# A twelve-block network on one core: layernorms by the statistics instruction, a rearranged delta rule, and narrow attention on single PSUM banks

## The chip, the core and the metric

The kernel runs on one core of a Trainium2 chip, in one launch. The metric is device time in microseconds for one execution, from inputs in HBM to the output in HBM. All arithmetic of interest here is float32.

## What is computed

A batch of 4 sequences of 128 tokens with 128 channels, `x`, goes through twelve blocks; each takes the layernorm of `x` and adds its result to `x`. A context of 4 x 2048 positions with 96 channels feeds three cross attentions. In order:

1. an attention and feed-forward with ternary weights and rounded inputs (`bit_attention`),
2. a selective state space block (`mamba`),
3. a grouped feed-forward,
4. a cross attention with 12 heads (`ctx_attention`),
5. the delta rule block (`rwkv`),
6. a mixture of 8 experts (`moe`),
7. a cross attention with 8 heads,
8. a causal attention with position biases (`alibi_attention`),
9. a ternary feed-forward (`bit_ffn`),
10. a cross attention with 8 heads of 16 channels (`narrow_attention`),
11. a causal attention with one head,
12. a routed feed-forward with gates.

The delta rule is the block with most of the change. Cut to what matters:

```python
x = _ln(x, ln_pre_w, ln_pre_b); xn = _ln(x, ln_attn_w, ln_attn_b)
dx = _shift(xn) - xn                       # xr, xw, xk, xv, xa, xg = xn + dx * x_r, ...
r, k, v = xr @ W_r, xk @ W_k, xv @ W_v
w_log = -softplus(-(w0 + tanh(xw @ w1) @ w2)) - 0.5
a = sigmoid(a0 + xa @ a1 @ a2);  g = sigmoid(xg @ g1) @ g2
kk = (k * k_k).reshape(.., 16, 8);  kk = kk / max(norm(kk), 1e-12)     # per head
k = k * (1.0 + (a - 1.0) * k_a)
def step(state, inp):                      # one token; state is 8 x 8 per head
    sa = einsum('bhij,bhj->bhi', state, a_t)          # a_t = -kk
    state = state * d_t + sa * b_t + v_t * k_t        # d = exp(-exp(w_log)), b = kk * a
    return state, einsum('bhij,bhj->bhi', state, r_t)
o = group_norm_of_heads(o) * gn_w + gn_b
o = o + (r * k * r_k).sum(head) * v
x = x + (o * g) @ W_o
xf = _ln(x, ln_ffn_w, ln_ffn_b); kf = xf + (_shift(xf) - xf) * ffn_x_k
x = x + square(relu(kf @ W_ffn1)) @ W_ffn2
```

A layernorm takes (x - mean) / sqrt(var + eps) over the last axis, times a weight and plus a bias where there are any. In `moe`, `bit_ffn` and `rwkv` a layernorm without weights is followed directly by one with weights.

## The kernel before

Tokens lie on the 128 partitions and (batch, channel) along the free axis, so `x` is a tile of 128 x 512; `transposed` turns it by four TensorE transposes into one PSUM bank and copies it out, with channels on the partitions. `copy` alternates between ScalarE and VectorE.

The program is written with pools of tiles. A pool has a number of buffers for each tag, and the tiles of one tag go round in them. Pools that are closed give their memory to the pools opened after them, in SBUF and in PSUM (8 banks of 512 float32 per partition). Every wait between engines comes from tiles that are written, read or given up. The order on each engine is set by a list scheduler: it follows the order of the program, but lets a later instruction go ahead where an earlier one isn't ready by its own estimate. Weights are loaded by SP through a pool of two buffers, a block ahead (`nxt()`).

**Layernorm** (`layernorm`, L330 to L351): sum (DVE, L335), mean (L337), centred copy (L339), square (POOL, L341), sum (L343), root (ACT, L345), reciprocal (L347), product (L348), and with weights two more passes (L350, L351).

**Delta rule** (`rwkv`): 784 to 973.6 us of the profile. Three layernorms; `transposed`; `shifted` copies the transpose into a padded tile and subtracts; six mixtures (`mixed`) each feed a matrix product (`mm`, tag "mm", four banks). The keys' head lengths go through a sum over heads and a reciprocal of all 512 columns (L1412). The sequence is cut in 32 blocks of 4 tokens (`NB`, `Q`). `products` (L1464) multiplies two operands, on DVE or POOL, in tag "pr" (two buffers) and sums over heads on PE. `spread` copies one of the 8 state columns to all channels of its head by a product with a constant. Tiles `br`, `ae` and `pt` hold what the 32 steps need; each step is four small DVE operations (L1545 to L1550) that depend on one another. Then the output: products of r with kh and v (L1554, `oa`), of r with be and `sa` (L1564), and for each of 8 columns `spread(rh, j)` times the state at the block's start (`oz`, also in tag "pr"), summed in `o_ps` by four products with the identity (L1584). After that come the group norm (a call of `layernorm`), its weights, the bonus term (`bo_ps`, `bs`, `vtok`), the gate `g`, W_o, and the feed-forward.

**Narrow attention**: keys kT and values v of one batch are projected from the transposed context (`project`, 8 key products of 512 columns, 16 value products of 136). For each batch b and each half of the heads s (four heads, one per group of 32 partitions), `maxima` computes all scores, four heads x 512 columns at a time, and reduces them on DVE (L709, L714); the row maxima are transposed (`m_tr`, L720) and added to the queries. `weighted` then computes transposed scores (L733, `t_ps`), takes the exponential on ACT (L739) and sums values on PE (L746, `av`), in four steps of four chunks. The loop runs `weighted` of (b, s) beside `maxima` of the next half and `project` of the next batch, one step of each in turn; `finish` normalises and multiplies by W_o. All score and projection tiles share tag "sc": three double banks. Small transposes have a bank of their own ("mi").

Of the kernel before, what the change touches and what calls it, by code (L numbers as in the profile page):

```python
# [18 lines left out]
P = 128  # L19
# [36 lines left out]
for _n, _w in [  # L56
    ("b_d2v", 1), ("b_img", 1), ("b_txt", 1), ("b_att0", 1), ("b_att1", 1), ("b_f1", 4),
    ("conv_w", 16), ("conv_b", 4), ("dtp_b", 4), ("D", 4), ("A_log", 64),
    ("x_r", 1), ("x_w", 1), ("x_k", 1), ("x_v", 1), ("x_a", 1), ("x_g", 1),
    ("w0", 1), ("a0", 1), ("k_k", 1), ("k_a", 1), ("r_k", 1), ("ffn_x_k", 1),  # L60
    ("moe_b1", 32), ("moe_gate", 8), ("b_q", 1), ("b_k", 1), ("b3_q", 1), ("b3_k", 1), ("router", 8), ("bq3", 2), ("inv_n", 7),
]:
    COLS.add(_n, _w)
# [3 lines left out]
for _n, _w in [  # L67
    ("b_f2", C), ("ln_pre_w", C), ("ln_pre_b", C), ("ln_attn_w", C), ("ln_attn_b", C),
    ("ln_ffn_w", C), ("ln_ffn_b", C), ("gn_w", C), ("gn_b", C), ("gamma", C), ("beta", C),
    ("b_v", C), ("b_out", C), ("ln1_g", C), ("ln1_b", C), ("ln2_g", 512), ("ln2_b", 512),  # L70
    ("b1", 512), ("b2", C), ("b3_v", C), ("bo1", C), ("bo2", C), ("bo3", C),
]:
    ROWS.add(_n, _w)
# [73 lines left out]
def _layout(i):  # L147
# [23 lines left out]
    for n in ("x_r", "x_w", "x_k", "x_v", "x_a", "x_g", "w0", "a0", "k_k", "k_a", "ffn_x_k"):  # L171
        col[n] = chunks(i["L1_attn_" + n])
    col["r_k"] = chunks(i["L1_attn_r_k"].reshape(-1))
# [12 lines left out]
    for n in ("ln_pre_w", "ln_pre_b", "ln_attn_w", "ln_attn_b", "ln_ffn_w", "ln_ffn_b", "gn_w", "gn_b"):  # L186
        row[n] = i["L1_attn_" + n]
    for n in ("gamma", "beta"):
        row[n] = i["L1_ffn_" + n]
# [81 lines left out]
class Net:  # L271
# [58 lines left out]
    def layernorm(self, pool, x, out, eps=0, w=None, b=None, tag="ln"):  # L330
# [3 lines left out]
        s = self.small(n, tag + "_s")  # L334
        nc.vector.reduce_sum(s, x, axis=AX)  # L335
        m = self.small(n, tag + "_m")
        nc.vector.tensor_scalar_mul(m, s, 1.0 / d)  # L337
        xc = pool.tile([P, n, d], F32, tag=tag + "_xc", name=tag + "_xc")
        nc.vector.tensor_sub(xc, x, bc_in(m, d))  # L339
        sq = pool.tile([P, n, d], F32, tag=tag + "_sq", name=tag + "_sq")  # L340
        nc.gpsimd.tensor_mul(sq, xc, xc)  # L341
        v = self.small(n, tag + "_v")
        nc.vector.reduce_sum(v, sq, axis=AX)  # L343
        sd = self.small(n, tag + "_sd")
        nc.scalar.activation(sd, v, AF.Sqrt, bias=self.eps[:, eps : eps + 1], scale=1.0 / d)  # L345
        r = self.small(n, tag + "_r")
        nc.vector.reciprocal(r, sd)  # L347
        nc.vector.tensor_mul(out, xc, bc_in(r, d))  # L348
        if w is not None:
            nc.vector.tensor_mul(out, out, bc_mid(w, n))  # L350
            nc.vector.tensor_add(out, out, bc_mid(b, n))  # L351

    def transposed(self, psum, pool, x, tag, dtype=F32):

        nc = self.nc
        ps = psum.tile([P, B, P], F32, tag="mm", name="tr_" + tag)
        for b in range(B):
            nc.tensor.transpose(ps[:, b], x[:, b], self.ident)  # L358
        out = pool.tile([P, B, P], F32, tag=tag, name=tag)
        self.copy(out, ps)  # L360
        return out

    def normed(self, psum, pool, tag="xn"):

        xn = pool.tile([P, B, C], F32, tag=tag, name=tag)
        self.layernorm(pool, self.x, xn)
# [90 lines left out]
    def ctx_attention(self, n, heads, mask, bo, nxt):  # L457
# [4 lines left out]
        with ExitStack() as es:  # L462
# [10 lines left out]
            self.layernorm(wk, self.x, xn)  # L473
# [154 lines left out]

    def narrow_attention(self, nxt):
# [7 lines left out]
        wqo, wkv = self.load("qo3"), self.load("kv3")  # L637
        scale = 1.0 / math.sqrt(ND)
        with ExitStack() as es:
# [7 lines left out]
            self.layernorm(one, self.x, xn)  # L647
            nc.vector.tensor_add(self.x, self.x, bc_mid(self.row("bo3"), B))
            tr = mi.tile([P, B, P], F32, tag="mi", name="tr_x")
# [24 lines left out]
            def project(b):  # L674

                kT = wk.tile([P, 2, S], F32, tag="kT", name="kT")
                v = wk.tile([P, NCH, NH * VW], F32, tag="v", name="v")
                for at in range(0, S, 512):
                    mm = ps.tile([P, 2, 512], F32, tag="sc", name="k_ps")
                    for s in range(2):  # L680
                        nc.tensor.matmul(  # L681
                            mm[:, s], wkv[:, s * P : s * P + P],
                            self.ctxT[: DC + 1, b * S + at : b * S + at + 512], start=True, stop=True)
                    self.copy(kT[:, :, at : at + 512], mm)
                    yield kT, v
                for c in range(0, NCH, 6):
                    mm = ps.tile([P, 2, 512], F32, tag="sc", name="v_ps")
                    n = min(6, NCH - c)
                    for j in range(n):
                        at = b * S + (c + j) * P  # L690
                        w = NH * VW
                        nc.tensor.matmul(
                            mm[:, j // 3, j % 3 * w : j % 3 * w + w], self.ctxT[: DC + 1, at : at + P],
                            wkv[:, 2 * P : 2 * P + w], start=True, stop=True)
                    for j in range(0, n, 3):
                        k = min(3, n - j)
                        self.copy(
                            v[:, c + j : c + j + k].rearrange("p c w -> p (c w)"), mm[:, j // 3, : k * w])
                    yield kT, v

            def maxima(b, s, kT):
# [3 lines left out]
                for j in range(4):  # L705
                    ts = [ps.tile([P, 2, 512], F32, tag="sc", name="s_ps") for _ in range(2)]
                    for g in (0, 2, 1, 3):
                        lo = g * 32
                        nc.tensor.matmul(  # L709
                            ts[g // 2][:, g % 2], qs[lo : lo + 32], kT[lo : lo + 32, s, j * 512 : j * 512 + 512],  # L710
                            start=True, stop=True)
                    for i, t in enumerate(ts):
                        at = j * 4 + i * 2
                        nc.vector.tensor_reduce(part[:, at : at + 2], t, axis=AX, op=ALU.max, negate=True)  # L714
                    yield
# [3 lines left out]
                tr = mi.tile([P, B, P], F32, tag="mi", name="m_tr")  # L719
# [5 lines left out]
            def weighted(b, s, kT, v, av):  # L725

                qs = q[:, s, b * T : b * T + T]
                for c0 in range(0, NCH, 4):
# [20 lines left out]

                    while late:  # L750
# [4 lines left out]
            def finish(b, av):  # L755
# [3 lines left out]
                tr = mi.tile([P, B, P], F32, tag="mi", name="o_tr")  # L759
# [7 lines left out]
                tr = mi.tile([P, B, P], F32, tag="mi", name="on_tr")  # L767
# [3 lines left out]
                y = mi.tile([P, B, P], F32, tag="mi", name="y")  # L771
# [9 lines left out]
            for kv in project(0):  # L781
                pass
            run(maxima(0, 0, kv[0]))
            done = None
            for b in range(B):
                av = avp.tile([P, 2, P], F32, tag="av", name="av")
                more = iter(project(b + 1)) if b + 1 < B else iter(())
                ahead = []
                for s in range(2):
# [4 lines left out]
                    for i, _ in enumerate(weighted(b, s, *kv, av)):  # L794
# [1223 lines left out]
```

## Time and profile before

| | |
|---|---|
| median of 3 runs | 1609.14 us (1604.18 to 1609.59) |
| profiled execution | 1603.5 us, span 1601.5 us, granted TensorE clock 0.842 |
| PE busy | 1180.8 us (74%) |
| DVE busy | 996.6 us (62%) |
| ACT busy | 625.3 us (39%) |
| POOL busy | 178.0 us (11%) |
| chain that ended last | PE 54%, DVE 15%, ACT 3% of the span |

A row of a group reads: line, engine, operation, output<-inputs, output form<-input form, count, then busy us and mean ns of one, then the engine's idle time just before it and what ended most of it. A row of the timeline reads: start in us, us, engine, line, operation, and in brackets the idle time before. A row of a window reads: its ends, its length, busy us (and number of instructions) of PE, PEld (weight loads), DVE, ACT and POOL, the granted clock, the DMA share and GB/s. Each float32 matmul appears as two records.

### The profile page before, as it was taken

What the parts mean: (1) busy time and instruction counts of PE and PEld (TensorE: products, weight loads), DVE (VectorE), ACT (ScalarE), POOL (GpSimd) and SP (SyncE); (2) the same over time, 40 slices, a digit from 0 to 9 for tenths busy, and PEclk for the clock granted to TensorE, in tenths of its full rate; (3) what the DMA queues carried; (4) which work ended last, traced back from release to release, by engine and by line L of the source; (5) the groups of instructions that cost most, each with busy time, mean ns of one, the idle gap of its engine ahead of it and who ended that gap; (6) DMA issues with size and microseconds to landing.
All of it is one profiled execution on the core that took longest, in us unless ns stands there. A gap on an engine that the chain in (4) does not pass through costs nothing.

```text
span 1601.5 us, 15594 instructions
## 1 busy us (share of the span) xinstructions
PE 1180.8 (74%) x6178; PEld 630.4 (39%) x6178; DVE 996.6 (62%) x1535; ACT 625.3 (39%) x786; POOL 178.0 (11%) x154
## 2 busy tenths in 40 slices
PE   2577356676999999999457055989775069989858
PEld 0266122224544444444223033754344035555534
DVE  8987478993376676676567954126676754344335
ACT  4722255551466565565333001436422113333242
POOL 0047023561000000000002000000030000000000
PEclk9988558798899999999759576989986578889778
DMA  5000000007000000000010005000000000000010
GB/s 163 1 2 2 0 1 26 1 0 192 1 0 1 0 1 0 0 0 1 0 53 0 0 1 155 1 20 0 2 1 9 0 1 2 1 1 2 6 50 7
DMA packets 9371, 28.19 MB, mean 18 GB/s; under 512 B 1175, under 2 KB 7104, under 8 KB 8142
## 3 DMA queue, kind: packets, MB, share of 16 engines
q1 hardware_dynamic: 8174, 24.88, 5.5%
q10 hardware_dynamic: 1120, 2.27, 0.4%
q8 instruction: 50, 0.82, 0.2%
q14 instruction: 27, 0.22, 0.0%
HBM read 26.88 MB, written 0.26 MB: 17 GB/s over the span
## 4 chain that ended last, share of the span: by engine, by line
PE 54%; DVE 15%; ACT 3%; issue 2%; POOL 1%; SPq 1%; DMA 1%; POOLq 0%; ACTq 0%; DVEq 0%
PE av L565 12%; PE sc L531 12%; PE s_ps L709 4%; DVE na_m L714 3%; PE mm L1361 3%; PE t_ps L733 3%; PE h_ps L1710 2%; PE av L746 2%; PE y_ps L1717 2%; PE q_ps L483 1%; PE o_ps L1782 1%; PE k_ps L681 1%; POOL ln_sq L341 1%; PE y L576 1%; DVE qa L1545 1%
## 5 line engine op out<-in xcount | busy, mean ns | idle before, releaser
L565 PE MATMUL av<-s,ctx 128*97 128x512 f32 x448 | 206.5, 597 | 6.6 <-ACT s L563 6.0
L531 PE MATMUL sc<-q_aug,ctxT 99*128 99x512 f32 x448 | 209.2, 593 | 0.0
L562 DVE TENSOR_TENSOR s<-s,mbs 128x1024 f32<-128x1024 f32 x112 | 132.3, 1217 | 38.8 <-ACT mbs L557 38.8
L533 ACT COPY s<-sc 128x1024 f32<-128x1024 f32 x112 | 113.0, 1009 | 96.6 <-PE sc L531 96.3
L714 DVE TENSOR_REDUCE na_m<-s_ps 128x2 f32<-128x1024 f32 x64 | 75.8, 1220 | 89.9 <-PE s_ps L709 89.6
L563 ACT ACTIVATE s<-s 128x1024 f32<-128x1024 f32 x112 | 115.4, 1056 | 35.7 <-DVE s L562 35.1
L541 DVE TENSOR_TENSOR m<-m,s 128x1024 f32<-128x1024 f32 x72 | 87.9, 1221 | 66.3 <-ACT s L533 66.3
L565 PEld LDWEIGHTS av<-s,ctx 128*97 128x97 f32 x448 | 73.1, 165 | 124.7 <-issue 105.9
L531 PEld LDWEIGHTS sc<-q_aug,ctxT 99*128 99x128 f32 x448 | 81.0, 189 | 88.0 <-issue 78.0
L1283 PE MATMUL y_ps<-hc,consts 128*128 128x512 f32 x128 | 75.4, 723 | 33.5 <-POOL hc L1281 30.6
L739 ACT ACTIVATE p<-t_ps 128x1024 f32<-128x1024 f32 x64 | 62.0, 1021 | 91.4 <-PE t_ps L733 91.4
L1281 POOL TENSOR_TENSOR hc<-h,cs 128x1024 f32<-128x1024 f32 x32 | 77.5, 2433 | 86.5 <-DVE h L1278 86.0
L341 POOL TENSOR_TENSOR ln_sq<-ln_xc 128x512 f32<-128x512 f32 (+1 forms) x19 | 23.3, 1227 | 566.2 <-DVE ln_xc L339 536.8
L1278 DVE TENSOR_TENSOR_SCAN h<-dA,dbu 128x512 f32<-128x512 f32 x64 | 74.4, 1203 | 3.6 <-ACT dA L1275 3.4
L709 PE MATMUL s_ps<-kT,q 32*128 32x512 f32 x256 | 65.3, 707 | 2.1 <-DVE na_m L714 1.1
L733 PE MATMUL t_ps<-q,kT 32*128 32x128 f32 x1024 | 56.3, 329 | 8.8 <-DVE na_m L714 5.8
L1283 PEld LDWEIGHTS y_ps<-hc,consts 128*128 128x128 f32 x128 | 25.9, 221 | 83.3 <-POOL hc L1281 57.0
L733 PEld LDWEIGHTS t_ps<-q,kT 32*128 32x128 f32 x1024 | 46.6, 223 | 27.1 <-DVE na_m L714 14.7
L1275 ACT ACTIVATE dA<-delta,A 128x508 f32<-128x508 f32 x64 | 42.7, 688 | 33.0 <-DVE h L1278 32.1
L345 ACT ACTIVATE ln_sd<-ln_v,eps 128x4 f32<-128x4 f32 (+1 forms) x19 | 5.7, 300 | 120.2 <-DVE ln_v L343 120.2
L1367 POOL MEMSET pad<- 128x4 f32 x2 | 0.2, 106 | 446.2 <-PE y L576 381.8
L358 PE MATMUL tr_xnT<-consts,xn 128*128 128x128 f32 x24 | 6.5, 428 | 54.3 <-DVE xn L348 35.5
(580 smaller groups left out, 2114.2 us busy)
## 6 DMA issues: line engine op xcount, KB each, us to landing
w_moe<-in_moe SPq DMA_DIRECT2D x2, 2048.0 KB, 8.5
ctxT<-in_ctxT SPq DMA_DIRECT2D x4, 768.0 KB, 13.1
rows<-in_rows ACTq DMA_DIRECT2D x1, 2048.0 KB, 13.4
w_l3f<-in_l3f SPq DMA_DIRECT2D x1, 1920.0 KB, 7.9
w_l0f<-in_l0f SPq DMA_DIRECT2D x1, 1024.0 KB, 4.8
w_mamba<-in_mamba SPq DMA_DIRECT2D x1, 976.0 KB, 20.1
w_r<-in_r SPq DMA_DIRECT2D x1, 960.0 KB
consts<-in_consts SPq DMA_DIRECT2D x1, 832.0 KB, 18.3
```

The costliest lines, as they stand in the source:

```text
L531: nc.tensor.matmul(sc[:, i], self.ctxT[:, at : at + P], u.q, start=True, stop=True)
L533: nc.scalar.copy(s, sc)
L541: nc.vector.tensor_max(u.m, u.m, u.s[j])
L562: nc.vector.tensor_sub(p, p, bc_mid(u.mb, 2))
L563: nc.scalar.activation(p, p, AF.Exp)
L565: nc.tensor.matmul(u.av[: DC + 1], self.ctx[:, u.b * NCH + chunks[2 * j + i]], p[:, i], start=j + i == 0, stop=j == n - 1 and i == 1)
L709: nc.tensor.matmul(ts[g // 2][:, g % 2], qs[lo : lo + 32], kT[lo : lo + 32, s, j * 512 : j * 512 + 512], start=True, stop=True)
L714: nc.vector.tensor_reduce(part[:, at : at + 2], t, axis=AX, op=ALU.max, negate=True)
L733: nc.tensor.matmul(ts[g // 2][:, g % 2, j], kT[g * 32 : g * 32 + 32, s, at : at + P], qs[g * 32 : g * 32 + 32], start=True, stop=True)
L1278: nc.vector.tensor_tensor_scan(h[:, half], self.flat(dA), dbu[:, half], 0.0, ALU.mult, ALU.add)
L1281: nc.gpsimd.tensor_mul(hc, h, bc_mid(cs, 2))
L1283: nc.tensor.matmul(y[:, half], self.ident, hc[:, half], start=n == 0, stop=n == 15)
```

## The change

Six parts:

- `layernorm` uses VectorE's statistics instruction (`bn_stats`, `bn_aggr`) per batch, then one scale-and-shift per batch; POOL has no part in it. `twice=True` does two layernorms in a row with one set of statistics and a second root. Layernorm weights that come ahead of a transpose are applied while the transpose is copied out, so they become columns (`ln_attn`, `ln_ffn`, `gamma`, `beta`).
- Delta rule, before the steps: the transpose goes straight into the padded tile (`mixing`); the gate's first product stands earlier; head lengths are summed to 16 columns, inverted there and transposed back; several copies and products change engine.
- Delta rule, after the steps: the spreads of `rh` are copied to SBUF and the gate and bonus terms are worked out on POOL ahead of the output sums (`beside`); the `oz` products stand before those of r with be; the sums are made against `centre` (identity minus one eighth of the head mask), so the heads' means are already taken away; the group norm is then a square, a sum and a root.
- `moe` and `bit_ffn` use `twice`; `bit_ffn` writes its second layernorm in place.
- Narrow attention: the keys and values of batches 0 and 1 are projected ahead of `bit_ffn` (`narrow_keys`), all copies on ScalarE; the weights kv3 have a pool of their own.
- In narrow attention's loop the scores for the maxima, the projections and the small transposes use three single banks (`sp`), the transposed scores two double banks; `maxima` yields after each head, and the loop takes two heads, then half a step of `weighted`, in turn.

```diff
@@ layernorm
-        nc.vector.reduce_sum(s, x, axis=AX)
...
-        nc.gpsimd.tensor_mul(sq, xc, xc)
...
+        for i in range(n):
+            nc.vector.bn_stats(st[:, i], x[:, i])
+        for i in range(n):
+            nc.vector.bn_aggr(mv[:, i], st[:, i])
+        r = first = self.root(mv[:, :, 1], "ln")
+        if twice:
+            v = self.small(n, "ln_v")
+            nc.vector.tensor_mul(v, mv[:, :, 1], r)
+            nc.vector.tensor_mul(v, v, r)
+            r = self.small(n, "ln_rr")
+            nc.vector.tensor_mul(r, first, self.root(v, "ln2"))
...
+        for i in range(n):
+            if w is None:
+                scaled(out, r, i)
+            else:
+                nc.vector.scalar_tensor_tensor(out[:, i], x[:, i], mv[:, i, 0:1], w, ALU.subtract, ALU.mult)
+                nc.vector.scalar_tensor_tensor(out[:, i], out[:, i], r[:, i : i + 1], b, ALU.mult, ALU.add)
@@ narrow attention: keys ahead
+    def narrow_keys(self, es):
+        pool = es.enter_context(self.tc.tile_pool(name="na_w", bufs=1))
+        self.wkv = pool.tile(list(self.A["kv3"].shape), F32, name="w_kv3")
+        self.nc.sync.dma_start(self.wkv, self.A["kv3"])
+        self.kvp = es.enter_context(self.tc.tile_pool(name="na_kv", bufs=2))
+        self.kv = {}
+        with self.tc.tile_pool(name="na_kvps", bufs=3, space=PSUM) as ps:
+            for b in range(2):
+                for self.kv[b] in self.project(ps, b, self.nc.scalar.copy):
+                    pass
...
-            ps = es.enter_context(tc.tile_pool(name="na_sc", bufs=3, space=PSUM))
-            mi = es.enter_context(tc.tile_pool(name="na_mi", bufs=1, space=PSUM))
+            ps = es.enter_context(tc.tile_pool(name="na_sc", bufs=2, space=PSUM))
+            sp = es.enter_context(tc.tile_pool(name="na_s", bufs=3, space=PSUM))
...
@@ maxima
-                    ts = [ps.tile([P, 2, 512], F32, tag="sc", name="s_ps") for _ in range(2)]
-                    for g in (0, 2, 1, 3):
...
+                    for g in range(4):
+                        t = sp.tile([P, 512], F32, tag="s", name="s_ps")
+                        rows = slice(g * 32, g * 32 + 32)
                         nc.tensor.matmul(
+                            t, qs[rows], kT[rows, s, j * 512 : j * 512 + 512], start=True, stop=True)
+                        at = j * 4 + g
+                        nc.vector.tensor_reduce(part[:, at : at + 1], t, axis=AX, op=ALU.max, negate=True)
+                        yield
@@ the loop
+                    steps = weighted(b, s, *kv, av)
+                    for i in range(NCH // 4):
+                        take(top, 2)
+                        next(steps)
+                        ahead = next(more, ahead)
+                        take(top, 2)
+                        next(steps)
+                        if done:
                             finish(*done)
                             done = None
...
                         ahead = next(more, ahead)
+                        if s == 0:
+                            ahead = next(more, ahead)
+                            ahead = next(more, ahead)
+                    take(top, 1)
@@ rwkv
-                nrm = tmp("nrm", pool=ta)
-                nc.scalar.activation(nrm, mm(self.k("heads"), sq), AF.Sqrt)
-                nc.vector.tensor_scalar_max(nrm, nrm, 1e-12)
+                lens = ps.tile([P, B, 16], F32, tag="mm", name="lens")
+                for b in range(B):
+                    nc.tensor.matmul(lens[:, b], sq[:, b * T : b * T + T], self.k("pick"), start=True, stop=True)
+                nrm = tmp("nrm", (P, B * 16), pool=ta)
+                nc.scalar.activation(nrm, self.flat(lens), AF.Sqrt)
                 nc.vector.reciprocal(nrm, nrm)
...
-                nc.vector.tensor_mul(rh, r, D)
+                nc.gpsimd.tensor_mul(rh, r, D)
...
-                    nc.scalar.copy(
+                    (nc.vector.tensor_copy if j % 2 else nc.scalar.copy)(
                         ae[:, :, :, :, j].rearrange("p n b q -> p b n q"),
...
+                def beside():
+                    sp = tmp("rsp", (P, 8, N), pool=tb)
+                    for j in range(8):
+                        nc.scalar.copy(sp[:, j], spread(rh, j))
...
+                    nc.gpsimd.tensor_mul(vh, vh, bc_in(bs, 8))
+                    nc.gpsimd.tensor_add(vtok, vtok, bc_mid(self.row("gn_b"), B))
+                    nc.gpsimd.tensor_mul(vtok, vtok, g)
+                    nc.gpsimd.tensor_mul(g, g, bc_mid(self.row("gn_w"), B))
+                    return sp
...
+                rsp = beside()
+                centre = tmp("centre", tag="k")[:, 0:P]
+                nc.vector.scalar_tensor_tensor(centre, self.k("heads"), -0.125, self.ident, ALU.mult, ALU.add)
...
+                for j in range(8):
+                    t = st.tile([P, B, NB, Q], F32, tag="pr", name="oz")
...
                 for s in range(Q):
...
                     products(rh, be, s, s, m, nc.gpsimd)
...
+                osq = tmp("osq", (P, B * 16, 8), tag="dec")
+                nc.scalar.activation(osq, oc, AF.Square)
+                o = tmp("o", (P, B, C), tag="nkk")
+                nc.vector.tensor_mul(o, o_ps, g)
+                v = self.small(B * 16, "rw_v")
+                nc.vector.reduce_sum(v, osq, axis=AX)
+                oh = o.rearrange("p b (h i) -> p (b h) i", i=8)
+                nc.vector.tensor_mul(oh, oh, bc_in(self.root(v, "rw", 1, 0.125), 8))
+                nc.vector.tensor_add(o, o, vtok)
...
@@ program
+            if BLOCKS[i][0] == "alibi_attention":
+                nes = es.enter_context(ExitStack())
+                net.narrow_keys(nes)
+            if BLOCKS[i][0] == "narrow_attention":
+                nes.close()
```

More of the change, by code (lines that the diff above doesn't have):

```diff
@@ L328, in small, with root, layernorm @@
         return self.st.tile([P, w], F32, tag=name, name=name)
-    def layernorm(self, pool, x, out, eps=0, w=None, b=None, tag="ln"):
+    def root(self, v, name, eps=0, scale=1.0):
+        nc = self.nc
+        n = v.shape[1]
+        sd = self.small(n, name + "_sd")
+        nc.scalar.activation(sd, v, AF.Sqrt, bias=self.eps[:, eps : eps + 1], scale=scale)
+        r = self.small(n, name + "_r")
+        nc.vector.reciprocal(r, sd)
+        return r
+    def layernorm(self, x, out, w=None, b=None, twice=False, inner=None):
@@ L343, in layernorm @@
[L343 to L353, printed above, removed]
-        nc = self.nc
[L356 to L360, printed above, removed]
+        st = self.small(6 * n, "ln_st").rearrange("p (n s) -> p n s", s=6)
@@ L672, in narrow_attention @@
             nxt()
[L674 to L699, printed above, removed]
             def maxima(b, s, kT):
@@ L779, in run, with take @@
                     gens = [g for g in gens if next(g, gens) is not gens]
-            for kv in project(0):
-                pass
-            run(maxima(0, 0, kv[0]))
+            def take(g, n):
+                for _ in range(n):
+                    if g is not None:
+                        next(g, None)
+            kv = self.kv[0]
+            take(maxima(0, 0, kv[0]), 17)
             done = None
@@ L1857, in quantized @@
                 return q, am
[L1859 to L1860 removed]
             xn = one.tile([P, B, C], F32, name="xn")
[L1862 removed]
+            self.layernorm(self.x, xn, w=self.row("ln1_g"), b=self.row("ln1_b"), twice=True)
             q, sc = quantized(xn, C, 0)
```

235 lines of the change are left out of this document (124 added, 111 removed).

## The prediction, before the run

> **What bounds the kernel now.** I read the page first: PE is busy 74% of the span and no engine is full, so each stage has to be read alone. Then came the layernorm lines, the windows and the timeline of the delta rule (784 to 973.6 us), the timeline of the two feed-forwards and of narrow attention (1231 to 1537 us), and the waits there.
>
> The page's layernorm square (busy, mean ns, idle before it and what ended it), then the timeline from one layernorm's start to the next one's:
> ```profile
> L341 POOL TENSOR_TENSOR ln_sq<-ln_xc 128x512 f32<-128x512 f32 (+1 forms) x19 | 23.3, 1227 | 566.2 <-DVE ln_xc L339 536.8
> ...
> 784.30 0.69 DVE L335 TENSOR_REDUCE ln_s<-x 128x4 f32<-128x512 f32 x1
> ...
> 789.07 0.69 DVE L335 TENSOR_REDUCE ln_s<-xn 128x4 f32<-128x512 f32 x1
> ```
> 19 layernorms, each 4.77 us of dependent steps over three engines, and PE waits behind most of them.
>
> The delta rule by stage: layernorms; projections; preparation; the 32 steps; output sums; group norm; feed-forward (length, then busy time by engine, granted clock):
> ```profile
> 784.00:802.00 18.00, 0.21 (x1) 0.24 (x2) 12.35 (x23) 0.89 (x3) 3.12 (x3) 0.54 0.00 0
> 802.00:830.00 28.00, 17.80 (x38) 6.34 (x37) 15.74 (x21) 14.36 (x17) 0.89 (x5) 0.62 0.21 75
> 830.00:865.50 35.50, 28.29 (x77) 13.74 (x78) 25.39 (x45) 13.57 (x17) 2.70 (x3) 0.86 0.00 0
> 865.50:914.00 48.50, 6.36 (x16) 2.24 (x15) 44.56 (x127) 0.00 (x0) 5.76 (x6) 0.63 0.00 0
> 914.00:938.00 24.00, 18.69 (x96) 12.77 (x96) 13.09 (x39) 0.94 (x2) 0.10 (x1) 0.83 0.00 1
> 938.00:951.00 13.00, 3.16 (x12) 2.50 (x12) 7.94 (x13) 1.27 (x2) 1.54 (x1) 0.55 0.00 0
> 951.00:973.60 22.60, 11.50 (x44) 6.97 (x44) 10.08 (x17) 3.89 (x7) 1.24 (x2) 0.66 0.05 9
> ```
> Only the steps fill an engine (DVE); elsewhere a chain sets the time.
>
> Waits inside the narrow loop (us in all, times, longest), and its first three batches:
> ```profile
> ACT p L739 <- PE t_ps L733: 91.4, 32, 12.7
> DVE na_m L714 <- PE s_ps L709: 89.0, 32, 6.8
> ...
> 1320.80:1374.10 53.30, 48.94 (x626) 29.43 (x626) 23.55 (x26) 19.75 (x23) 0.00 (x0) 0.90 0.01 2
> 1374.10:1431.10 57.00, 52.40 (x631) 30.00 (x631) 24.99 (x31) 20.02 (x24) 0.00 (x0) 0.88 0.01 1
> 1431.10:1489.30 58.20, 53.66 (x631) 31.01 (x631) 24.93 (x31) 20.02 (x24) 0.00 (x0) 0.85 0.02 5
> ```
> ACT and DVE wait for PE; PE waits for PSUM, since scores for maxima, scores for weights and projections share three double banks.
>
> **The change part by part** (times are this trace's; gains negative).
>
> *Single layernorms.* bn_stats is not in the trace. Its nearest row is the 128x128 reduce (L1770), two in 0.47 us, so four are 0.97; four bn_aggr like the 0.16 us operations on 128x4, overlapping, 0.45; root and reciprocal as now 0.65; four 128x128 scale-and-shift like L1768 (two in 0.48) 0.9. Sum 2.95, gain 1.8. Bounds: free statistics would give 1.5 us in all, statistics at twice the reduce 3.9. On the path stand five (mamba, grouped ffn, alibi, causal, routed): -9. In the two ctx attentions weight folding holds PE until 410.9 and 1062.2; I take -1 for the second, 0 for the first, and 0 for the opening, where DVE's input maxima lie between the steps. **-10** (-5 to -16). [...]
>
> *Delta rule.* (a) Three layernorms with weights take 784.30 to 801.7, 17.4. After: one with a second root (+1.15) and eight 128x128 operations with weights (2.4 in place of 0.9) 5.7, then a plain one: 8.7. **-8.7.** (b) Copying the transpose into the padding (0.62) goes: -0.65. (c) Projections: the 3.35 us reciprocal (L1412) becomes one of 64 columns (0.55, L347's wide form), table loads fall from six to four, kk's square moves to ACT; the head-length route gains 4 transposes (1.1). Walking PE, ACT and DVE from 805, the last use of this stage's pool falls near 823 instead of 829: **-5.8** (0 to -8). (d) rh on POOL takes 0.65 off DVE. (e) Half of the ae copies go to DVE, which is busy with vk until 860.2; behind them stand the dm matmuls, 1.84 us, then dend: -0.7. (f) The steps stay. Their cover is disturbed by POOL:
> ```profile
> 868.58 1.39 DVE L1545 TENSOR_TENSOR qa<-pt,ae 128x144 f32<-128x144 f32 x1
> ...
> 872.80 0.40 DVE L1545 TENSOR_TENSOR qa<-pt,ae 128x144 f32<-128x144 f32 x1
> ```
> The first runs beside a POOL product, the second alone; about 2 us are lost for 5.8 us of POOL now. Four gate operations come in (some 5 us of POOL), the four be products (4.3) go out: 0 (-1 to +2). (g) Output sums, 917.05 to 936.9. The spreads move beside the steps, where ACT and PE are idle (uncovered they would cost PE 8 x 0.86 = 7). But buffers go round in the order of the program:
> ```profile
> 859.01 2.41 POOL L1468 TENSOR_TENSOR pr<-r,kh 128x512 f32<-128x512 f32 x2 [20.93 <-DVE pt L1500]
> ```
> r and kh were ready at 837.6 and POOL idle, yet the product waited for the last vk to leave tag "pr". The oz tiles now precede the be products in that tag, so those, done at 872 today, run after the steps. PE does eight times four oz matmuls, 1.02 us each, three at half clock: 11 us; then POOL (1.36, 1.36, 0.8, 0.8), PE, DVE and the last four matmuls, 7 us more. 18.3 for 19.8: **-1.5** (-9 if the tag doesn't bind, +3). (h) Group norm, 936.9 to 946.2, 9.3: now square 0.6, sum 0.69, root 0.35, reciprocal 0.55, two operations 0.69, gaps: 3.8. **-5.5.** (i) Feed-forward layernorm with weights 6.3 to 2.95, padding copy and last addition: -4.6. Sum **-28** (-15 to -40).
>
> *moe.* Two layernorms, 973.63 to 984.57; after, 4.1: **-6.8.**
>
> *bit_ffn.* Its second layernorm (1254.96 to 1273.42, 18.46) becomes four statistics and eight passes of 512 at about 0.7: 9.4, -9.1. Ahead of it the key projections of two batches now stand, in PSUM banks that bit_ffn's own pool takes over. Today:
> ```profile
> 1230.32 0.58 PE L1830 MATMUL tot<-bf_s,ones 128*128 128x2 f32 x2 [0.78 <-DVE x L1802]
> ...
> 1299.47 5.31 PE L681 MATMUL k_ps<-ctxT,w_kv 97*128 97x512 f32 x12
> 1304.62 3.87 PE L692 MATMUL v_ps<-w_kv,ctxT 97*128 97x136 f32 x32
> ```
> tot's input was ready long before; it waited for the last reader of the old pool's PSUM. So tot will wait for the last of 28 copies. w_kv3 is issued near 1229.6 on SP when alibi's memory is free (w_qo queues behind it, harmless) and lands 2.4 us later; then 16 k matmuls of 0.885 and twice 3.87 for v, 21.9, and 3.5 for half clock at the start: done near 1258.5. tot, the weights' quantization (2.7) and then h_ps, queued behind it on PE, at 1261.8 instead of 1248.1: +13.7. ACT's 28 copies (15.4) hide under PE. **+4.6.**
>
> *Narrow attention, before its loop* (1287.0 to 1320.85). Layernorm -2.4 (5.4 now). The first projection (1296.2 to 1308.4) is gone; 16 maxima of 512 in place of 8 of 1024: 10.4 for 9.7. **-11.5.**
>
> *Its loop* (1320.85 to 1532, 211). Four row groups run side by side today; a lone one, at half clock, and a quartet at full clock:
> ```profile
> 1378.15 2.07 PE L709 MATMUL s_ps<-kT,q 32*128 32x512 f32 x2
> ...
> 1390.15 1.14 PE L709 MATMUL s_ps<-kT,q 32*128 32x512 f32 x8
> ```
> So four cost what one costs, 1.07. In the change two are issued, then t_ps or av: 2.14 per step. PE work at full clock, now: 28 x 1.1 + 32 x 1.1 + 32 x 1.1 + 3 projections of 11 = 134, so 77 of the 211 are waits and half clock. After: 28 x 2.14 + 70.4 + 2 x 11 = 152. Half clock takes about 15% of 211, 32, now; I take 23. The three finishes and eight m_tr chains (about 2 and 6 us) stay partly, 18; the bank waits go, because t_ps has two double banks of its own. 193, **-18** (-40 to +20). DVE (112 reduces of 0.66, 74 us) and ACT (64 exponentials of 0.97, 62, and copies, 18) stay under it. kv3 leaves the weights' slots, so l3a can load earlier; nothing waits for it today.
>
> Sum: -10 - 28 - 6.8 + 4.6 - 11.5 - 18 = -70. The profiled execution took 1603.5 (span 1601.5), the median is 1609.1: 1533.5 to 1539, I say 1536. Under 0.5%, 8 us, nothing could be told from no change.
>
> **The rivals.**
> 1. *The banks don't hold bit_ffn*: the projections then hide under DVE's layernorms; +13.7 becomes about -4: 1518. Against it tot's row.
> 2. *The loop doesn't shrink*: pairs and three single banks make PE wait as today; loop 211 to 230: 1554 to 1574. For it the 2.14; against it the 89 and 91 us of waits that a bank of its own removes.
> 3. *Slower: half clock through the loop.* The granted clock is 0.85 to 0.90 in three batches, and at half wherever PE pauses (0.50 in 1230 to 1258). If pairs of row groups and short waits keep it at half, 152 becomes 304, the loop about 340: 1683. It decides once the loop passes 263 us, a clock under 0.68. Against it: sparser work ran at 0.88. [...]
> 4. *Better*: the be products don't wait and half clock leaves the loop, -7 and -25: 1504.
>
> **How the numbers follow.** Forecast 0.5, rival 1 0.18, rival 2 0.2, rival 3 0.05, rival 4 0.07. Faster by over 0.5% in all but rival 3 and a sliver of rival 2. The range runs from rival 4, with 8 us more out of the delta rule's bounds, to rival 2's end with the layernorms' worst, 5 more: 1496 to 1579; 1 in 10 is left on either side at most.
>
> **What would show it.** Right: layernorms near 3 us, no POOL square; POOL pr with kb after the last step; tot released by the last v copy, near 1217 in new time; s_ps in pairs of about 1.07; a loop near 193. Wrong: tot soon after alibi; a loop over 211; half clock throughout; bn_stats over 0.5 us each.

## The result, and the profile after

The changed kernel takes 1516.54 us (median of 4 runs, 1514.26 to 1518.61), against 1609.37 us of before in the same comparison: a ratio of 0.943, 95% interval 0.9405 to 0.9455. Its profiled execution took 1514.3 us with a span of 1512.2 us and a granted clock of 0.873. That profiled execution is the fastest of the four. The forecast was 1536 us, with a range of 1496 to 1579; the span fell by 89.3 us where the sum said 70.

By stage (from the moment `x` is ready to the next such moment; narrow's loop begins at its first `t_ps`), us:

| stage | before | after | moved | forecast |
|---|---|---|---|---|
| up to the delta rule | 784.3 | 784.9 | +0.6 | -3.6 |
| delta rule | 189.3 | 165.0 | -24.4 | -28 |
| moe | 84.1 | 77.6 | -6.5 | -6.8 |
| second ctx attention, alibi | 173.3 | 171.1 | -2.2 | -2.8 |
| bit_ffn | 56.0 | 58.9 | +2.9 | +4.6 |
| narrow, before its loop | 33.9 | 26.0 | -7.9 | -11.5 |
| narrow, loop and last finish | 216.9 | 172.1 | -44.8 | -18 |
| causal, routed | 63.7 | 56.7 | -7.0 | -3.6 |

Narrow's loop gave 26.8 us more than its term; the other rows together gave 7.2 less than theirs.

*A layernorm*, VectorE's timeline at mamba's (start, length, the operation, idle time before it):
```profile
180.59 0.29 DVE L351 BATCH_NORM_STATS2 ln_st<-x 128x6 f32<-128x128 f32 x1
...
181.48 0.37 DVE L353 BATCH_NORM_AGGREGATE ln_mv<-ln_st 128x2 f32<-128x6 f32 x4
182.21 0.18 DVE L338 RECIPROCAL ln_r<-ln_sd 128x4 f32<-128x4 f32 x1 [0.36 <-ACT ln_sd L336]
182.42 1.12 DVE L363 TENSOR_SCALAR xn<-x,ln_mv,ln_r 128x128 f32<-128x128 f32 x4
```
From 180.59 to 183.54 it is 2.95 us, the forecast's figure, and POOL has no part in it.

*The delta rule by stage*, windows of the kernel after: layernorms, projections, preparation, steps, output sums, group norm, feed-forward (length, then busy time of PE, PEld, DVE, ACT, POOL, granted clock, DMA):
```profile
784.90:791.10 6.20, 0.61 (x3) 0.55 (x3) 5.13 (x25) 0.89 (x3) 0.00 (x0) 0.66 0.00 0
791.10:816.80 25.70, 20.18 (x47) 8.72 (x45) 10.72 (x17) 13.45 (x17) 1.66 (x3) 0.55 0.23 82
816.80:853.40 36.60, 28.63 (x77) 13.88 (x78) 29.25 (x49) 10.62 (x15) 4.50 (x8) 0.91 0.00 0
853.40:906.10 52.70, 10.74 (x33) 5.20 (x32) 48.19 (x137) 4.90 (x9) 6.33 (x6) 0.65 0.00 0
906.10:922.60 16.50, 14.11 (x80) 11.36 (x80) 8.62 (x16) 0.00 (x0) 3.84 (x4) 0.89 0.00 0
922.60:927.10 4.50, 0.00 (x0) 0.00 (x0) 3.22 (x5) 0.94 (x2) 0.10 (x1) 0.59 0.00 1
927.10:949.90 22.80, 14.97 (x56) 9.56 (x56) 9.55 (x24) 2.69 (x5) 1.54 (x3) 0.63 0.00 1
```
Cut at the same events, before has 17.4, 27.3, 36.6, 51.5, 19.9, 9.3 and 27.4 us. Layernorms, output sums, group norm and feed-forward shrank; projections hardly, and the preparation not at all.

*Two waits that the prediction named*, from the timelines of POOL and PE after, and one that it did not, from VectorE's:
```profile
914.76 2.33 POOL L1528 TENSOR_TENSOR pr<-r,kb 128x512 f32<-128x512 f32 x2 [45.02 <-PE o_ps L1654]
...
1226.98 0.38 PE L1902 MATMUL tot<-bf_s,ones 128*128 128x2 f32 x2 [0.53 <-ACT v L695]
...
1208.83 0.18 DVE L338 RECIPROCAL ln_r<-ln_sd 128x4 f32<-128x4 f32 x1 [8.08 <-ACT ln_sd L336]
```
The be products did wait for the `oz` products to leave tag "pr", and `tot` for the last copy of the early values, at 1226.98 where the forecast had 1217. The third line is new: ACT's root for bit_ffn's first layernorm stood behind key copies that waited for w_kv's transfer (5.72 us on PE) and PE.

*Narrow's loop*, its second and third batch (columns as above):
```profile
1327.90:1376.40 48.50, 46.73 (x633) 28.67 (x632) 23.63 (x43) 23.56 (x34) 0.00 (x0) 1.00 0.01 2
1376.40:1423.80 47.40, 45.78 (x633) 28.56 (x633) 23.68 (x45) 23.21 (x33) 0.00 (x0) 1.00 0.01 2
```
PE is busy 96% at full clock; before, these stretches were 57 and 58 us long at 0.88 and 0.85. The loop up to its last finish, before and then after:
```profile
1320.85:1532.00 211.15, 191.66 (x2414) 115.48 (x2417) 84.86 (x100) 75.56 (x88) 0.00 (x0) 0.84 0.01 2
```
```profile
1283.42:1449.60 166.18, 157.67 (x2367) 100.23 (x2369) 81.80 (x147) 80.67 (x102) 0.00 (x0) 0.98 0.01 2
```
PE's idle time fell from 19.5 to 8.5 us. Counted up to the last product with W_o in the trace's record of the granted clock, half clock fell from 66.0 to 7.5 us. The profile above is at the short end: in seven profiles with this loop as changed (after, `own_banks`, `split`, `be_tag`, `lens`, `best`, `gffn_old`), the loop up to that product takes 171.3 to 180.4 us (216.1 before), with 7.5 to 25.4 us at half clock.

### The profile page after: what moved, and what is told of

Its sections match the earlier page's. It is cut to its first block, busy times and chain, and to the rows that moved or that the text cites. A ratio compares the mean times of both kernels' runs of the same rounds, so it can differ in the third digit from the quotient of the medians.

```text
span 1512.2 us, 15752 instructions
## 1 busy us (share of the span) xinstructions
PE 1173.2 (78%) x6186; PEld 631.2 (42%) x6188; DVE 960.0 (63%) x1664; ACT 638.4 (42%) x825; POOL 163.5 (11%) x143
## 4 chain that ended last, share of the span: by engine, by line
PE 63%; DVE 22%; ACT 6%; issue 4%; POOL 2%; DMA 2%; SPq 1%; DVEq 0%; ACTq 0%; another core or an unknown queue 0%; POOLq 0%
PE av L596 13%; PE sc L562 13%; PE s_ps L751 5%; PE mm L1413 3%; DVE h L1331 3%; PE t_ps L773 2%; PE h_ps L1782 2%; PE y_ps L1789 2%; PE k_ps L681 2%; PE y_ps L1336 2%; PE q_ps L514 2%; PE av L786 1%; POOL hc L1334 1%; PE o_ps L1854 1%; DVE dbu L1322 1%
## 5 line engine op out<-in xcount | busy, mean ns | idle before, releaser
L754 DVE TENSOR_REDUCE na_m<-s_ps 128x1 f32<-128x512 f32 x128 | 82.6, 687 | 64.2 <-PE s_ps L751 64.2
L751 PE MATMUL s_ps<-kT,q 32*128 32x512 f32 x256 | 83.0, 696 | 1.6 <-DVE na_m L754 1.6
L1328 ACT ACTIVATE dA<-delta,A 128x508 f32<-128x508 f32 x64 | 42.7, 689 | 33.1 <-DVE h L1331 32.1
L1654 PE MATMUL o_ps<-centre,oz 128*128 128x128 f32 x64 | 9.8, 322 | 41.6 <-DVE oz L1650 41.6
L1793 DVE SCALAR_TENSOR_TENSOR x<-y_ps,cw,x 128x128 f32<-128x128 f32 x32 | 9.0, 345 | 51.0 <-PE y_ps L1789 51.0
L1322 DVE TENSOR_TENSOR dbu<-du,b_ps 128x1024 f32<-128x1024 f32 x32 | 37.7, 1208 | 2.0 <-PE b_ps L1307 1.8
## 6 DMA issues: line engine op xcount, KB each, us to landing
rows<-in_rows ACTq DMA_DIRECT2D x1, 1664.0 KB, 12.3
```

Source lines behind the costliest of these rows:

```text
L751: nc.tensor.matmul(t, qs[rows], kT[rows, s, j * 512 : j * 512 + 512], start=True, stop=True)
L754: nc.vector.tensor_reduce(part[:, at : at + 1], t, axis=AX, op=ALU.max, negate=True)
```

## Experiments

Every time below is a median beside runs of the kernel before on the same chip; stage times are from each run's profile.

### What made narrow's loop short

`old_loop`: three shared double banks, four heads per step and copies on both engines, as before.
```diff
-                        t = sp.tile([P, 512], F32, tag="s", name="s_ps")
...
+                    ts = [ps.tile([P, 2, 512], F32, tag="sc", name="s_ps") for _ in range(2)]
...
```


> The changed kernel with the narrow attention's loop of before (three double banks for all score and projection tiles, four heads per step, copies on both engines); the keys of batches 0 and 1 still come ahead of bit_ffn. Theory A, banks and order made the loop short: the loop goes from 168 back to about 200 (211 less one projection of 11), PE pauses of about 2.1 us return at the batch boundaries and half clock for 14 to 17 us after each; 1516.5 + 32 = 1549 us. Theory B, the loop is short because only two projections are left in it: loop about 175, 1524 us.

Measured 1548.5 us (ratio to before 0.965, 0.9634 to 0.9666), as theory A has it. The loop up to the last product with W_o is 206.3 us for 171.3, with 63.0 us at half clock. PE at the second batch boundary, first `old_loop`, then the first boundary of the kernel after:
```profile
1382.02 0.33 PE L789 MATMUL m_tr<-consts,nmx 128*128 128x128 f32 x1 [2.11 <-DVE nmx L786]
1382.73 0.60 PE L802 MATMUL t_ps<-q,kT 32*128 32x128 f32 x4 [0.38 <-DVE q L790]
```
```profile
1325.29 0.41 PE L802 MATMUL o_tr<-consts,o 128*128 128x128 f32 x2 [1.08 <-DVE o L326]
1325.63 0.50 PE L773 MATMUL t_ps<-q,kT 32*128 32x128 f32 x8
```
In the old order the last maxima of a half are reduced while PE has nothing else, and `m_tr` makes it wait 2.11 us. The record then shows 17.1 us at half clock (1382.4 to 1399.5). In the new order matmuls stand between, and the longest pause at a batch boundary is 1.08 us. From the loop's first `t_ps` until `x` is ready, `old_loop` takes 207.1 us for 172.1: half clock costs 31.9 us for 4.1, PE is idle for 27.3 us for 11.6, and PE's own work, reckoned at full clock, is 8.4 us less. Banks, order and copies went back together, so their shares are not told apart.

`keys_inside`: all four projections back in narrow attention.
```diff
-            kv = self.kv[0]
+            for kv in self.project(sp, 0, nc.scalar.copy):
+                pass
```


> The changed kernel with all four projections inside narrow attention (batch 0 before its loop, batch 1 in it); loop, banks and order as changed. Theory A, banks and order made the loop short: bit_ffn loses its wait (about -12.5 us), the stretch before the loop gets about 12 us, the loop 11 us of PE work at full clock (168 to about 179): 1527 us. Theory B, the projections taken out of the loop made it short: loop over 200, 1551 us.

1524.4 us (0.9497, 0.9479 to 0.9514): theory A again, so banks, order and copies are worth 32 us and the early keys 8. The parts differ from what was expected: bit_ffn takes 37.7 us, 21 less than after, not 12.5; the loop is 23 us longer, not 11. The loop's first batch, now with a projection, runs at 0.81.

`pause`, `pause6`, `pause12`: PE's pause at the boundary is lengthened by 3, 6 and 12 passes of VectorE; nothing else changes.
```diff
+                for _ in range(3):
+                    nc.vector.tensor_scalar_mul(o, o, 1.0)
```


> The changed kernel with three passes more of VectorE over the normalisation tile o (times 1.0) in each of the four finishes of narrow attention, so that PE's pause at a batch boundary grows from 1.08 to about 2.2 us. Theory A, a pause of about 2 us sends the granted clock to half for some 14 us: each of three boundaries costs 1.1 + 7.5 us, the last finish 1.1: 1516.5 + 27 = 1543 us, and the clock's record shows 0.5 after each boundary. Theory B, the clock follows how dense the work is over a longer time: only the passes are paid, 4.4 us, 1521 us, clock 1.0 throughout.

> As the kernel pause, with six passes over o instead of three: PE's pause at a batch boundary about 3.0 us. Theory A, the longer the pause the surer the half clock: all three boundaries are followed by 14 to 20 us at half clock, each costing 2 + 8 us, the last finish 2: 1516.5 + 32 = 1548 us. Theory B, chance alone (where the boundary falls): one of three as with 2.04 us, 1516.5 + 8 + 10 = 1534 us.

> As the kernel pause, with twelve passes over o: PE's pause at a batch boundary about 5.0 us. Theory A, the longer the pause the surer the half clock: after all three boundaries, each costing 4 + 8 us, the last finish 4: 1516.5 + 40 = 1556 us. Theory B, the clock does not follow single pauses: only the passes are paid, 1516.5 + 16 = 1532 us.

1528.3, 1533.1 and 1549.0 us. In `pause` the boundaries' pauses were 2.04, 2.04 and 1.81 us, followed by 20.5, 0 and 6.8 us at half clock. The stretch behind the first one, and an equal one after it:
```profile
1322.80:1343.20 20.40, 20.28 (x66) 7.93 (x67) 3.84 (x9) 5.52 (x9) 0.00 (x0) 0.50 0.00 1
1343.20:1363.60 20.40, 20.23 (x291) 13.57 (x289) 9.53 (x17) 9.75 (x15) 0.00 (x0) 1.00 0.01 2
```
PE is busy 99% in both and still at half clock for the whole of the first. `pause6` (2.80, 2.80, 2.58 us) was followed by 6.8, 0 and 10.2 us, nearer to theory B. In `pause12` the pause did not become 5 us: other products were moved into it, and it stayed 2.14 us with one of 0.83 ahead of it twice; 20.5, 6.8 and 17.1 us followed, and half clock in the loop is 70.4 us. So neither theory holds alone. A pause of about 2 us brings half clock back, but not each time, and its length from 2 to 3 us does not order the outcomes. Over all profiles here, 16 of 18 boundary pauses of 1.8 us or more were followed by half clock within 7 us, and 5 of 24 of about 1 us.

### Where bit_ffn waits

`own_banks`: the projections' pool is kept open, so bit_ffn gets other banks.
```diff
-        with self.tc.tile_pool(name="na_kvps", bufs=3, space=PSUM) as ps:
+        self.kvps = ExitStack()
+        ps = self.kvps.enter_context(self.tc.tile_pool(name="na_kvps", bufs=3, space=PSUM))
```


> The changed kernel with the PSUM banks of the early key projections kept open through bit_ffn, so that bit_ffn has other banks; the program's order is unchanged. Theory of the first rival, the shared banks are what holds bit_ffn: its first layernorm and h_ps go ahead while the projections hide: about -18, 1499 us. Theory of PE's order: tot goes ahead, but the 22 us of projections still stand before q_tr on PE, so only the quantization of the weights (2.7 us of VectorE after tot) comes off the path: about -3, 1513.5 us.

1517.3 us (1509.9 to 1523.7): not told apart from the kernel after. The stage settles it: bit_ffn 55.7 us for 58.9, the 3 us of the second theory. PE's timeline:
```profile
1210.69 0.28 PE L1903 MATMUL tot<-bf_s,ones 128*128 128x2 f32 x2
...
1227.99 0.39 PE L1937 MATMUL q_tr<-identb,q 128*128 128x128 bf16 x4
```
`tot` goes ahead, `q_tr` still stands behind all projections though its input was ready at 1218.1. The first rival of the prediction (without a wait for banks the projections hide, -18) is refuted. In this profile (an execution of 1523.7 us) what bit_ffn gained was lost in narrow's loop, where half clock came to 23.9 us.

`split`: banks of its own, eight pieces ahead, the rest after bit_ffn's second layernorm in the program.
```diff
+        self.keys = both()
+        for _ in range(8):
+            next(self.keys)
...
             self.layernorm(h, h, w=self.row("ln2_g"), b=self.row("ln2_b"))
+            for _ in self.keys:
+                pass
...
```


> The changed kernel with banks of their own for the early projections, and with only the first 8 key products issued ahead of bit_ffn in the program, the other 20 pieces after bit_ffn's second layernorm, where PE is idle for 18.7 us. Forecast: h_ps follows the end of batch 0's projection (about 1219 us instead of 1230.7) and the rest lies under VectorE's layernorm: -11, 1505.5 us. Rival: the pieces under the layernorm hold ACT's root or PE's q_tr by as much as they save: 0, 1516.5 us.

1505.1 us (0.9366, 0.9332 to 0.94): bit_ffn 47.2 us, 11.7 less than after.
```profile
1219.83 0.60 PE L1948 MATMUL h_ps<-qw,qT 128*128 128x512 bf16 x2
...
1242.18 1.71 PE L1960 MATMUL q_tr<-identb,q 128*128 128x128 bf16 x12 [9.85 <-DVE q L1933]
```
`h_ps` comes 19 us after `x` is ready (32 in the kernel after), and PE's hole ahead of the second `q_tr` is 9.85 us instead of 18.7: the projections lie in it.

### The delta rule

`be_tag`: the be products in buffers of their own.
```diff
-                    products(rh, be, s, s, m, nc.gpsimd)
+                    products(rh, be, s, s, m, nc.gpsimd, ("dec", "nkk")[s % 2])
```


> The changed kernel with the four products of r with be (POOL, pr with kb) in buffers of their own (the free tiles dec and nkk) instead of tag pr. Theory: they waited for the oz products only because of the buffers; now they run beside the steps, and the 6 us of POOL, PE and VectorE after the last oz go: output sums 16.4 to about 11, the steps lose about 1.5 to POOL: -4, 1512.5 us. Rival: they run late anyway, or POOL slows the steps by as much: 1516.5 us.

1512.9 us (0.9417, 0.9397 to 0.9438): by the time not told apart from the kernel after. In the profile the output sums take 10.4 us for 16.5, and the whole delta rule 156.2 for 165.0; 2.6 us of that fall in the projections, which this edit does not touch (see `lens`). POOL's timeline has the first of these products before the steps:
```profile
850.21 1.09 POOL L1528 TENSOR_TENSOR pr<-r,kb 128x384 f32<-128x384 f32 x1 [2.26 <-PE mm L1413]
```
The tag was the cause of the late products; the steps take 0.5 us more, beside POOL.

`lens`: the head-length products right after the square.
```diff
                 nc.vector.tensor_copy(k, k_ps)
 
+                lens = ps.tile([P, B, 16], F32, tag="mm", name="lens")
+                for b in range(B):
+                    nc.tensor.matmul(lens[:, b], sq[:, b * T : b * T + T], self.k("pick"), start=True, stop=True)
...
-                lens = ps.tile([P, B, 16], F32, tag="mm", name="lens")
-                for b in range(B):
-                    nc.tensor.matmul(lens[:, b], sq[:, b * T : b * T + T], self.k("pick"), start=True, stop=True)
```


> The changed kernel with the four head-length products (lens) issued right after the square of the keys instead of after the gate's product. Theory: the delta rule's projections end late because the head-length chain (lens 806.7, root 808.9, reciprocal, transposes 810.2, kb 812.1, then six ACT operations queued behind the one that waits for kb) starts late; ds comes 3 us earlier, less 1.3 for one more table load: -2, 1514.5 us. Rival: PE at half clock and the four banks of tag mm set the end: 0 or slower by the table load, 1516.5 to 1518 us.

1518.1 us (1514.5 to 1523.1): inconclusive by the time. In its profile `ds` comes 29.7 us after `x` is ready for 31.9, and the block takes 162.7 us, as the theory has it. But four profiles without this edit (`keys_inside`, `pause6`, `be_tag`, `gffn_old`) have `ds` at 29.3 to 29.4 us too, with 13.7 to 17.1 us of that at half clock for 27.3 in the kernel after, so the gain is not shown to come from the edit. The root of the head lengths starts 8.1 us earlier (15.9 us after `x` is ready for 24.0), yet `kb` ends only 0.9 us earlier (27.0 for 27.8): an early start of this chain alone does not bring `kb` forward. The span is the same, with half clock over the whole span at 426 us for 384.

`best`: `split`, `be_tag` and `lens` together.
```diff
+            for _ in self.keys:
+                pass
...
+                    products(rh, be, s, s, m, nc.gpsimd, ("dec", "nkk")[s % 2])
...
+                    nc.tensor.matmul(lens[:, b], sq[:, b * T : b * T + T], self.k("pick"), start=True, stop=True)
```


> The three edits split, be_tag and lens together. If each brings what is expected and they do not touch one another: -11 - 4 - 2, 1499.5 us.

1498.8 us, ratio 0.9323 (0.9299 to 0.9346), against the changed kernel's 0.9405 to 0.9455: faster than the kernel before and the kernel after, by 17.7 us than the latter by the medians. It is not told apart from `split` alone (0.9332 to 0.94).

### What the layernorms alone bring

`ln_only`: the kernel before with the statistics layernorm and nothing else.
```diff
-        nc.gpsimd.tensor_mul(sq, xc, xc)
...
+            nc.vector.bn_stats(st[:, i], x[:, i])
```


> The kernel before with the statistics layernorm alone (no double layernorms, the group norm of the delta rule as before, weights as rows; nothing else of the change). By the forecast's terms: single layernorms -10 and narrow's -2.4; three with weights in the delta rule and one in moe and bit_ffn, 6.2 to about 4.4 each, and the plain ones of moe and bit_ffn 1.8 each: -12.6; bit_ffn's second -9.1: 1609 - 34 = 1575 us. By the trace after, mamba's and the grouped feed-forward's are given back at the weight folding of the first cross attention: 1579 us.

1556.4 us (0.9691, 0.9659 to 0.9723): -49, where the terms gave -30 to -34. By stage: delta rule -12.3, moe -6.1, second ctx attention and alibi -4.6, bit_ffn -15.0, narrow -9.9, causal and routed -6.7, up to the delta rule +4.6. In narrow's loop half clock came to 47.1 us for 66.0; that is worth 9.5 us, nearly all of narrow's gain, and the edit leaves the loop as it was, so this part may be chance.

`gffn_old`: the kernel after with the old layernorm in the grouped feed-forward alone.
```diff
-            xT = self.flat(self.normed(ps, wk))
+            xn = wk.tile([P, B, C], F32, tag="xn", name="xn")
+            self.groupnorm(wk, self.x, xn, tag="gl")
+            xT = self.flat(self.transposed(ps, wk, xn, "xnT"))
```


> The changed kernel with the layernorm of before in the grouped feed-forward alone (4.77 us instead of 2.95). Forecast's step: this layernorm is on the path, +1.8 us, 1518.3 us, and the first scores sc of the cross attention start 58.0 us after r_qk is issued. Theory from the trace after: the folding of that attention's weights starts when r_vo lands, 27.2 us after the issue of r_qk at mamba's end, however short the feed-forward is: sc starts 56.2 us or less after the issue, as now, 1516.5 us.

The total, 1522.4 us (1517.1 to 1533.8), says nothing at this size. The place does: PE's first product with r_vo, kernel after, then `gffn_old`:
```profile
396.71 0.33 PE L470 MATMUL a_ps<-r_vo,r_qk 64*99 64x1 f32 x2 [2.60 <-DMA r_vo<-in_vo]
```
```profile
398.60 0.25 PE L493 MATMUL a_ps<-r_vo,r_qk 64*99 64x1 f32 x2
```
With the short layernorm PE reaches the folding early, waits 2.60 us for `r_vo` (issued at 385.60, behind `r_qk`, whose issue began at mamba's end, at 369.50), and folds mostly at half clock (0.68 up to the first `sc`); with the long one it does not wait (0.79). From the issue of r_qk to the first `sc` it is 56.2 us after (54.3 to 57.6 in the other profiles with the short layernorm) and 52.3 with the longer one. The forecast's +1.8 is refuted as far as one profile goes: there the shorter layernorm gained nothing, and the way to the first `sc` is 2 to 5 us longer with it, with 17.1 to 20.5 us at half clock for 10.2.

## Why the prediction was right, and where its terms were off

*Single layernorms* (forecast -10): 2.95 us each, as estimated. The failed step is the count of those on the path: mamba's and the grouped feed-forward's were given back at the weight folding (first product with r_vo 3.1 us earlier than before, first `sc` 0.3 later), and the stage ahead of mamba took 1.6 us more: +0.6 in place of -3.6. Causal and routed gave 3.4 more than their two terms, 2.4 of it in causal. By the timeline three of causal's four statistics are taken at 1327.86, 1376.44 and 1423.79, as narrow finishes each batch, and PE's first transpose comes 1.6 us after `x` is ready for 5.0, as soon as one batch is scaled; the sum had priced the length of a layernorm, not when it can start and when its first part is done.

One statistics operation alone takes 0.29 us (mamba's first, at 180.59 in the profile after), but four in a row take 0.87 (the delta rule's second layernorm, at 788.20), not four times 0.29; the forecast had 0.97 for four.

*Delta rule* (-28, measured -24.4). (a) -11.2 for -8.7: three batches' statistics and first weighting were taken inside the attention ahead. (b) and (c) -1.6 for -6.5, the mis-sized term. Half of the miss is half clock: in the four profiles named at `lens` this stretch is 2.5 to 2.6 us shorter. Table loads (1.28 us each) fell to five, not four. The walk ended the projections by the engines' work, but by ACT's timeline five operations, `ds` the last, stand behind one that waited 3.8 us for `kb`; what that queue costs is not shown. (d) and (e) 0 for -1.35. (f) +1.2 for 0, inside its bounds. (g) -3.4 for -1.5: the be products came late by the tag, as said. (h) -4.8 for -5.5, (i) -4.6 as forecast.

*moe* -6.5 for -6.8.

*bit_ffn* (+4.6, measured +2.9) came out as added up: the first `h_ps` comes 32.1 us after `x` is ready for 17.1, +15.0 for +13.7; the second layernorm took 8.1 us for 18.5, -10.4 for -9.1; and the way from `h_ps` to that layernorm is 1.8 shorter, which the sum had not. What the sum hides is the price: `keys_inside` has bit_ffn without the early projections at 37.7 us (first layernorm pair and weights' quantization 6.8 us for 13.0), so the projections cost 21 us there, nearly all their PE time. The mechanism was half right: `tot` waited for the banks as said, but `own_banks` shows that PE's order alone would have held `q_tr`.

*Before the loop* -7.9 for -11.5: the sixteen maxima ran mostly at half clock (0.57 in 1257.4 to 1282.5).

*The loop* (-18, measured -44.8) is the mis-sized term. The half clock of before was sized rightly (66 us of it, 33 lost; the sum had 32), but 23 was kept for after, and 3.7 was measured (3.7 to 12.7 in the seven profiles above: the size of the gain is in part luck, its direction is not). That was the half of the fourth rival with -25. The step that failed is "I take 23": half clock was taken as a share of the loop, where the trace of before showed it starting within 3 us of each 2.11 us pause of `m_tr` (PE's timeline, then a window of the same kernel):
```profile
1373.73 0.33 PE L720 MATMUL m_tr<-consts,nmx 128*128 128x128 f32 x1 [2.11 <-DVE nmx L717]
...
1376.10:1389.80 13.70, 13.70 (x71) 5.77 (x74) 3.06 (x5) 3.83 (x6) 0.00 (x0) 0.50 0.00 1
```
The change's order removes that pause. The second mis-sized term is the 18 kept for pauses: PE is idle for 8.5 us. The 152 of PE work held (155 by the trace, at full clock), but the 134 for before did not: it is 159, so waits and half clock were 52 of the 211, not 77. Smaller slips: the terms for the early keys add up to 1257.4, not 1258.5, and the 3.5 us for half clock at their start was an estimate (after, half clock ends 3.9 us behind the first key product, and the first eight products take 9.35 us, the second eight 7.03); the fourth rival takes off 25 where the sum had kept 23; and the third rival's limit of 263 us means, with its own 152 and 18, a clock of 0.65, not 0.68. The third rival, half clock through the loop, did not come: with three single banks in rotation, and no pause over 1.08 us up to the last finish, the record of the kernel after stays at full clock for 163.8 us.

## What to carry to other kernels

Before pricing a loop on PE, lay the pauses of PE beside the record of the granted clock: one wait of 2.1 us at a boundary was followed by 13 us at half clock on average (nine cases of the old order), some 7 us lost, and the new loop, whose order puts independent matmuls there, was worth 32 us. When work is moved ahead of another stage, look at the order of PE's and ACT's queues as well as at banks. And a statistics operation per batch may start its layernorm before the last batch is there (three of causal's four did), while a shorter layernorm gained nothing where PE then waited for a transfer (2.60 us for `r_vo`, in one profile).

## What the runs showed of the hardware

In the records of before and after the granted clock has two values only, 0.5 and 1.0, and changes in steps of 3.41 us. Behind a pause at a batch boundary half clock lasted 3.4 to 20.5 us where it came, though PE was busy 99% in the longest of these stretches. Pauses of about 2.1 us were followed by half clock in all 9 cases of the old order (before, `old_loop`, `ln_only`), and the return to full clock took up to six steps (20.5 us, in `pause` and `pause12`). What decides between 0 and 20.5 us behind equal pauses stays open. Total half clock came to between 377 and 445 us in profiles of kernels that differ from the changed one by one experiment's edit, which is why edits of 2 or 3 us could not be read in the total. A stage can move as much without an edit: the delta rule up to `ds` took 31.9 us with 27.3 at half clock, or 29.3 with 13.7, in kernels that are alike there. So a stage's gain of that size needs its waits, or more than one profile, beside it.
